# Reordered loads and weight folds, products of zeros ahead of the first load, and last sums chunk by chunk, in an FFT-attention and fp8 feed-forward kernel

## The chip, the cores and the metric

The kernel runs on one core of a Trainium2 chip. The metric is the time of one execution on the device in microseconds (us). A profile is of one such execution; its span is a little shorter than the execution's own time. In the profile PE is TensorE (matmuls), PEld its weight loads, DVE VectorE, ACT ScalarE, POOL GpSimd, and SP the engine that issues most DMAs.

## The reference

Four batches of 512 tokens of width 512 (x is 4x512x512, float32). First an attention without softmax, with 16 heads of 32 values:

```python
h = layernorm(x)
q  = (h @ W_q.T).reshape(B, S, 16, 32);  kv = (h @ W_kv.T).reshape(B, S, 16, 32)
qf = fft(q);  kvf = fft(kv)             # along a head's 32 values
qf = qf / l2norm(qf);  kvf = kvf / l2norm(kvf)
kvf = cumsum(kvf, axis=1)               # along the tokens of a batch
y = x + ifft(qf * kvf).real.reshape(B, S, 512) @ W_o.T
```

Then a feed-forward layer of inner width 1536, with weights rounded to fp8 (e4m3):

```python
h = layernorm(y)
g = silu((h @ fp8(gate_w)) * gate_scale);  u = (h @ fp8(up_w)) * up_scale
out = y + ((g * u) @ fp8(down_w)) * down_scale
```

## The kernel before, in words

The work is cut into 16 chunks of 128 tokens (N = 16, four to a batch). Nothing reorders it: the program is written out by hand, each engine executes its instructions in the order in which the Python code emits them, and Tile adds the semaphore waits.

**Loads.** SP issues in turn the first table `fwd` (L98), two of the four 128-row blocks of W_kv, the chunk x of 0, the identity table (L123), the other two blocks of W_kv, the transposed chunk xT of 0, then W_q, x and xT of 1, two more tables, and W_o (L115 to L130).

**Folds.** The real FFT is folded into the weights. `fold_in` (L162) multiplies 128x128 blocks of W_kv (tiles `pkv`) and W_q (tiles `pw`) by `fwd`: 16 products each, which PE executes as 32 instructions. `folded` (L172) copies the four sums to SBUF, two on ACT and two on DVE. `fold_out` (L176) folds the inverse transform into W_o in four 128x512 products, 8 instructions. Before, PE's order is W_kv, a quarter of W_q, chunk 0's `spectrum` with W_kv, the rest of W_q, W_o, and chunk 0's `spectrum` with W_q.

**A round of the attention.** For a chunk i:

- `x_mean`, `x_deviation` (ACT, with one power on POOL) give the layernorm; `x_row` (PE, L356) and `x_center` (DVE, L360) subtract the mean from xT;
- `spectrum(i, 1)` and `spectrum(i, 0)` (PE, L368, 8 instructions each) form k and q in the frequency domain; `squared` (ACT, L379), `summed` (DVE, L384) and `norms` (POOL, L389) their norms;
- `k_scaled` (DVE, L392) scales k and adds the carry of the chunk before; ACT copies the rounded high part `kh`, and `k_low` (DVE, L414) the remainder `kl`;
- `running` (PE, L423) sums along the tokens with a triangular matrix into `cum`; `carry` (ACT, L430, L431) copies the last row and sends it by a DMA to the next chunk; `q_scaled`, `products` (DVE, L440, L441) and `combined` (POOL, L449, L450) multiply the spectra;
- `v_out`, `v_back` take the product through DRAM, `v_turn` (DVE, L330) transposes it, `project` (PE, L467) multiplies it by the folded W_o, and `finish` (DVE, L475) adds x.

Chunks 0 to 2 are written out in a prologue (L601 to L684); the loop at L688 has one round for each of chunks 3 to 15, in which PE executes the two spectra of i, the running sum of i - 1 and the projection of i - 3.

**Rounding the weights.** The feed-forward weights come in 36 units, each rounded by ACT (`quant_abs`, L214) and by three or four parts on DVE (`next_parts`, L267): step, (floor), add and sub. `given` (L687) says how many parts a round has: 3 or 2. The prologue has four.

**Feed-forward.** 48 steps, 12 to a batch: `inner` (L532) forms 512 gate and up sums (16 matmuls each, `gu`), the product `f`, its rounded high part `fh` (ACT) and the remainder `fl` (DVE); `down` (L562) adds the step's share to four sums `pd`, one to a chunk, with 8 matmuls. For the last two steps `down` goes chunk by chunk. At a batch's end each chunk is scaled (DVE, L583), the residual added (POOL, or DVE for half of the last batch, L585) and stored (L586).

Of the kernel before, what the change touches and what calls it, by code (L numbers as in the profile page):

```python
# [15 lines left out]
P = 128  # L16
# [19 lines left out]
def tile_fft_attention_then_fp8_ffn(  # L36
# [54 lines left out]
    XB = 7  # L91
# [3 lines left out]


    tab = const.tile([P, 4, P], F32, name="tab")
    nc.sync.dma_start(tab[:, 0, :], tables[:, 0, :])  # L98
    fwd, ident, inv, tri = (tab[:, i, :] for i in range(4))

    xt, xTs = {}, {}
# [1 line left out]
    def load_xT(i):  # L103
        xTs[i] = work.tile([P, KC, P], F32, tag="xT", name=f"xT_{i}", bufs=3)
        nc.sync.dma_start(xTs[i], xT[i])

    def load_x(i):
        b, c = chunks[i]
        t = work.tile([P, D], F32, tag="x", name=f"x_{b}_{c}", bufs=XB)
        nc.sync.dma_start(t, x[b, c * P : (c + 1) * P, :])  # L110
        xt[i] = t
# [5 lines left out]
    for i, w in enumerate((w_kv, w_q, w_oT)):  # L117
        t = big_tile(f"raw{i}")
        for j in range(KC):
            nc.sync.dma_start(t[:, j, :], w[j * P : (j + 1) * P, :])  # L120
            if (i, j) == (0, 1):
                load_x(0)
                nc.sync.dma_start(tab[:, 1, :], tables[:, 1, :])  # L123
        raw.append(t)
        if i == 0:
            load_xT(0)
        elif i == 1:
            load_x(1)
            load_xT(1)
            nc.sync.dma_start(tab[:, 2:, :], tables[:, 2:, :])  # L130
# [28 lines left out]
    wq = big_tile("wq")  # L159
    wo = big_tile("wo")  # L160

    def fold_in(pw, r, j):  # L162
        for i in range(KC):
            nc.tensor.matmul(  # L164
                pw[i][:, j * P : (j + 1) * P],
                lhsT=r[:, j, i * P : (i + 1) * P],
                rhs=fwd,
                start=True,
                stop=True,
            )  # L170

    def folded(w, pw):  # L172
        for i in range(KC):
            (nc.scalar.copy, nc.vector.tensor_copy)[i % 2](w[:, i, :], pw[i])

    def fold_out(w, r):  # L176
        for j in range(KC):
            pw = ps.tile([P, D], F32, tag="acc", name="pw", bufs=4)
            nc.tensor.matmul(pw, lhsT=inv, rhs=r[:, j, :], start=True, stop=True)  # L179
            (nc.vector.tensor_copy, nc.scalar.copy)[j % 2](w[:, j, :], pw)  # L180


    U1 = 12
# [110 lines left out]

    def deviation(src, less, name):

        rstd = work.tile([P, 1], F32, tag="dev", name=f"dev_{name}", bufs=6)
        each = work.tile([P, D], F32, tag="each", name=f"each_{name}", bufs=1)
        nc.scalar.activation(each, src, AF.Square, bias=less, accum_out=rstd)  # L299
        nc.scalar.activation(rstd, rstd, AF.Identity, scale=1.0 / D, bias=eps)  # L300
        nc.gpsimd.tensor_tensor(rstd, rstd, nhalf[:, 0:1], ALU.pow)  # L301
        return rstd
# [40 lines left out]
    def x_mean(i):  # L343
        st_x[i] = lesses[i] = mean(xt[i], nm(i))
# [5 lines left out]
    def x_stats(i):  # L350
        x_mean(i)
        x_deviation(i)

    def x_row(i):
        rows[i] = ps.tile([P, KC, P], F32, tag="tp", name=f"row_{nm(i)}")
        nc.tensor.transpose(rows[i][:, 0, :], lesses[i].to_broadcast([P, P]), ident)  # L356

    def x_center(i):
        row = rows.pop(i)[:, 0:1, :].to_broadcast([P, KC, P])
        nc.vector.tensor_tensor(xTs[i], xTs[i], row, ALU.add)  # L360
# [51 lines left out]
    def k_low(i):  # L412
        kn, kh, kl = kns[i]
        nc.vector.tensor_tensor(kl, kn, kh.bitcast(F32), ALU.subtract)  # L414
# [113 lines left out]

    fused, pds = {}, {}
    STEPS = B * MC  # L530

    def inner(n, on_pe, on_act, between):  # L532
        b, m = divmod(n, MC)
        pgu = []
        for j, w in enumerate((wg, wu)):
            p = ps.tile([P, S], F32, tag="b", name=f"gu{j}_{b}_{m}")
            for k in range(KC):
                for v in (yhs[b], yls[b]):
                    nc.tensor.matmul(  # L539
                        p,  # L540
                        lhsT=w[:, k, m * P : (m + 1) * P],
                        rhs=v[:, k, :],
                        start=k == 0 and v is yhs[b],
                        stop=k == KC - 1 and v is yls[b],
                    )
            pgu.append(p)
            if j == 0:
                on_pe(n, 0)
        g = work.tile([P, S], F32, tag="tmp", name=f"g_{b}_{m}")
        nc.scalar.activation(g, pgu[0], AF.Silu, scale=gus[:, 0, m : m + 1])  # L550
        f = work.tile([P, S], F32, tag="qn", name=f"f_{b}_{m}")
        nc.vector.scalar_tensor_tensor(f, pgu[1], gus[:, 1, m : m + 1], g, ALU.mult, ALU.mult)  # L552
        on_act(n)
        fh = work.tile([P, S], F32R, tag="kh", name=f"fh_{b}_{m}", bufs=3)
        fl = work.tile([P, S], F32R, tag="kl", name=f"fl_{b}_{m}", bufs=3)
        nc.scalar.copy(fh, f)  # L556
        between(n)
        nc.vector.tensor_tensor(fl, f, fh.bitcast(F32), ALU.subtract)  # L558
        fused[n] = (fh, fl)
        on_pe(n, 1)  # L560

    def down(steps):  # L562

        b = steps[0] // MC
        if steps[0] % MC == 0:
            pds[b] = [
                ps.tile([P, D], F32, tag="acc", name=f"pd_{b}_{c}", bufs=4) for c in range(TC)
            ]
        for c in range(TC):
            for n in steps:  # L570
                m = n % MC
                for v in fused[n]:
                    nc.tensor.matmul(  # L573
                        pds[b][c],
                        lhsT=v[:, c * P : (c + 1) * P],
                        rhs=wd[:, m, :],
                        start=m == 0 and v is fused[n][0],
                        stop=m == MC - 1 and v is fused[n][1],
                    )
        if steps[-1] % MC == MC - 1:  # L580
            for c in range(TC):
                o = work.tile([P, D], F32, tag="x", name=f"o_{b}_{c}", bufs=XB)
                nc.vector.tensor_tensor(o, pds[b][c], dsc, ALU.mult)  # L583
                add = nc.vector if b == B - 1 and c % 2 else nc.gpsimd
                add.tensor_tensor(o, o, ys[b][:, c, :], ALU.add)  # L585
                nc.sync.dma_start(out[b, c * P : (c + 1) * P, :], o)  # L586


    def pair(n):
# [3 lines left out]
    def at(f, i, *more):  # L593
        if 0 <= i < N:
            f(i, *more)

    pkv = [ps.tile([P, D], F32, tag="acc", name=f"pkv{i}", bufs=4) for i in range(KC)]
    for j in range(KC):
        fold_in(pkv, raw[0], j)
    x_stats(0)  # L600
    x_row(0)  # L601
    folded(wkv, pkv)
    x_center(0)
    pw = [ps.tile([P, D], F32, tag="b", name=f"pw{i}") for i in range(2)]
    pw.append(ps.tile([P, D], F32, tag="tp", name="pw2"))
    pw.append(ps.tile([P, D], F32, tag="acc", name="pw3", bufs=4))
    fold_in(pw, raw[1], 0)
    x_stats(1)
    nc.vector.tensor_copy(tri_r, tri)

# [5 lines left out]
    spectrum(0, 1)  # L616
    squares(0, 1)
    norms(0, 1)
    for j in range(1, KC):
        fold_in(pw, raw[1], j)  # L620
    folded(wq, pw)
    x_row(1)
    x_center(1)
    quant_abs(0)
    k_scaled(0)
    fold_out(wo, raw[2])
    k_low(0)
    next_parts(1, True)
    spectrum(0, 0)
    squared(0, 0)  # L630
    running(0)
    carry(0)
    x_stats(2)
    next_parts(1, True)
    summed(0, 0)
    norms(0, 0)

    dsc = const.tile([P, D], F32, name="dsc")
    nc.sync.dma_start(gus[:, 0, :], gate_scale)
# [1 line left out]
    nc.sync.dma_start(dsc, down_scale.partition_broadcast(P))  # L641
    load_x(3)
    load_xT(3)
    spectrum(1, 1)
    squared(1, 1)
    x_row(2)
    x_center(2)
    summed(1, 1)
    norms(1, 1)
    q_scaled(0)  # L650
    products(0)
    combined(0)
    load_unit(wanted.pop(0))
    load_unit(3)
    v_out(0)
    spectrum(1, 0)
    squared(1, 0)
    x_mean(3)
    summed(1, 0)
    k_scaled(1)  # L660
    k_low(1)
    norms(1, 0)

    load_xT(4)
    load_x(4)
# [1 line left out]
    x_row(3)  # L667
    squared(2, 1)
    x_deviation(3)
    summed(2, 1)  # L670
    norms(2, 1)
    x_center(3)
    spectrum(2, 0)
    running(1)
    squared(2, 0)
    carry(1)
    x_mean(4)
    q_scaled(1)
    products(1)
    combined(1)  # L680
    v_back(0)
    summed(2, 0)
    norms(2, 0)
    next_parts(2, True)  # L684


    given = [2 if i in (6, 8, 10, 11, 12) else 3 for i in range(N - 3)] + [1, 0, 0]  # L687
    for i in range(3, N):  # L688

        at(load_xT, i + 2)  # L690
# [76 lines left out]
    def behind(n):  # L767
# [24 lines left out]
        if b + 1 < B and 0 <= m - 3 < TC:  # L792
            y_deviation(b + 1, m - 3)


    for n in range(STEPS + 1):
        if n < STEPS:
            inner(n, on_pe, on_act, between)
        if n == STEPS:
            down([n - 2, n - 1])  # L800
        elif n == STEPS - 1:
            down([n - 2])
        elif 0 < n < STEPS - 2:
            down([n - 1])
        if n < STEPS:
            behind(n)


def _tables():
# [61 lines left out]
```

## Time and profile before

| | |
|---|---|
| time, 3 runs | 464.65 to 465.56 us, median 465.56 us |
| the profiled execution's own time | 465.4 us |
| its span | 463.6 us |
| PE busy | 452.5 us (98%) in 1672 instructions |
| DVE busy | 280.9 us (61%) |
| ACT busy | 211.9 us (46%) |
| POOL busy | 192.6 us (42%) |
| spectrum, 8 instructions | 3.43 us of PE, one start to the next |
| one round of the attention, chunks 5 to 12 | 10.88 us of PE |
| one step of the feed-forward | 5.44 us of PE |

The profile lists for each engine its instructions with their start and length. A PE instruction is listed until its pipeline is empty, so a matmul's cost in a stream is the distance from its start to the next start. Times in the timeline count from the span's start.

### The profile page before, as it was taken

What the parts mean: (1) busy time and instruction counts of PE and PEld (TensorE: products, weight loads), DVE (VectorE), ACT (ScalarE), POOL (GpSimd) and SP (SyncE); (2) the same over time, 40 slices, a digit from 0 to 9 for tenths busy, and PEclk for the clock granted to TensorE, in tenths of its full rate; (3) what the DMA queues carried; (4) which work ended last, traced back from release to release, by engine and by line L of the source; (5) the groups of instructions that cost most, each with busy time, mean ns of one, the idle gap of its engine ahead of it and who ended that gap; (6) DMA issues with size and microseconds to landing.
All of it is one profiled execution on the core that took longest, in us unless ns stands there. A gap on an engine that the chain in (4) does not pass through costs nothing.

```text
span 463.6 us, 5026 instructions
## 1 busy us (share of the span) xinstructions
PE 452.5 (98%) x1672; PEld 308.5 (67%) x1672; DVE 280.9 (61%) x387; ACT 211.9 (46%) x428; POOL 192.6 (42%) x134
## 2 busy tenths in 40 slices
PE   6999999999999999999999999999999999999995
PEld 6544344444444444777788888888888888888883
DVE  1539898999888688798996342344433333522225
ACT  3663665656688433246943225533235432222220
POOL 0248888888899886510262140022301021400002
PEclk9999999999999999999999999999999999999999
DMA  8734366667645633662341050430141420200002
GB/s 290 278 113 137 91 159 160 183 178 216 193 126 154 163 77 85 189 207 91 101 105 23 0 182 22 92 69 0 45 138 30 100 53 1 91 1 0 0 1 90
DMA packets 82586, 49.13 MB, mean 106 GB/s; under 512 B 62080, under 2 KB 62464, under 8 KB 82560
## 3 DMA queue, kind: packets, MB, share of 16 engines
q1 hardware_dynamic: 82176, 48.79, 36.8%
q8 instruction: 13, 0.21, 0.2%
q14 instruction: 13, 0.11, 0.1%
q10 hardware_dynamic: 384, 0.03, 0.1%
HBM read 33.04 MB, written 15.73 MB: 105 GB/s over the span
## 4 chain that ended last, share of the span: by engine, by line
PE 92%; DVE 3%; ACT 3%; issue 1%; DMA 1%; ACTq 0%; SPq 0%; DVEq 0%
PE gu L539 38%; PE pq L368 19%; PE pd L573 19%; PE po L467 11%; PE cum L423 1%; PE pkv L164 1%; PE pw L179 1%; ACT sq L379 1%; PE pw L164 1%; ACT qm L222 1%; DMA raw<-in_w_kv 1%; ACT each L299 0%; ACT qa L221 0%; PE pt_f L317 0%; DVE ss L384 0%
## 5 line engine op out<-in xcount | busy, mean ns | idle before, releaser
L389 POOL TENSOR_TENSOR rn<-ss,nhalf 128x16 f32<-128x16 f32 x32 | 103.6, 3238 | 16.3 <-DVE ss L384 13.8
L552 DVE SCALAR_TENSOR_TENSOR f<-gu,gus,g 128x512 f32<-128x512 f32 x48 | 36.0, 750 | 108.5 <-PE gu L539 103.4
L539 PE MATMUL gu<-yh,wg 128*128 128x512 f32 x192 | 76.5, 398 | 0.0
L573 PE MATMUL pd<-wd,fl 128*128 128x512 f32 x192 | 74.8, 389 | 0.0
L539 PE MATMUL gu<-yl,wg 128*128 128x512 f32 x192 | 74.8, 389 | 0.0
L539 PE MATMUL gu<-yh,wu 128*128 128x512 f32 x192 | 74.7, 389 | 0.0
L573 PE MATMUL pd<-wd,fh 128*128 128x512 f32 x192 | 74.7, 389 | 0.0
L539 PE MATMUL gu<-yl,wu 128*128 128x512 f32 x192 | 74.7, 389 | 0.0
L556 ACT CAST fh<-f 128x512 fp32r<-128x512 f32 x48 | 29.8, 620 | 80.4 <-DVE f L552 80.4
L368 PE MATMUL pq<-wkv,xT 128*128 128x512 f32 x128 | 57.9, 595 | 1.3 <-DVE xT L360 1.3
L550 ACT ACTIVATE g<-gu,gus 128x512 f32<-128x512 f32 x48 | 33.0, 687 | 56.7 <-PE gu L539 56.4
L467 PE MATMUL po<-wo,qvT 128*128 128x512 f32 x128 | 57.6, 593 | 0.1
L368 PE MATMUL pq<-wq,xT 128*128 128x512 f32 x128 | 57.6, 592 | 0.0
L558 DVE TENSOR_TENSOR fl<-f,fh 128x512 fp32r<-128x512 f32 x48 | 35.8, 745 | 27.5 <-ACT fh L556 27.5
L585 POOL TENSOR_TENSOR o<-o,ys 128x512 f32<-128x512 f32 x14 | 17.7, 1291 | 81.7 <-DVE o L583 72.7
L368 PEld LDWEIGHTS pq<-wkv,xT 128*128 128x128 f32 x128 | 24.0, 190 | 31.1 <-issue 27.2
L301 POOL TENSOR_TENSOR dev_f<-dev_f,nhalf 128x1 f32<-128x1 f32 x16 | 12.5, 781 | 72.1 <-ACT dev_f L300 72.0
L368 PEld LDWEIGHTS pq<-wq,xT 128*128 128x128 f32 x128 | 23.2, 190 | 28.0 <-issue 27.2
L539 PEld LDWEIGHTS gu<-yh,wg 128*128 128x128 f32 x192 | 36.0, 188 | 8.7 <-issue 0.5
L539 PEld LDWEIGHTS gu<-yl,wg 128*128 128x128 f32 x192 | 36.0, 188 | 8.3 <-issue 0.7
L573 PEld LDWEIGHTS pd<-wd,fl 128*128 128x128 f32 x192 | 36.0, 188 | 7.7 <-DVE fl L558 0.2
L539 PEld LDWEIGHTS gu<-yh,wu 128*128 128x128 f32 x192 | 36.0, 188 | 7.5
(89 smaller groups left out, 609.6 us busy)
## 6 DMA issues: line engine op xcount, KB each, us to landing
x<-in_x SPq DMA_DIRECT2D x16, 256.0 KB, 3.2
xT<-in_xT SPq DMA_DIRECT2D x16, 256.0 KB, 3.1
qv_all<-qv SPq DMA_DIRECT2D x16, 256.0 KB, 4.4
zv<-qv_all SPq DMA_DIRECT2D x64, 64.0 KB, 2.6
y_all<-x SPq DMA_DIRECT2D x16, 256.0 KB, 2.3
ys<-y_all SPq DMA_DIRECT2D x16, 256.0 KB, 3.4
out<-o SPq DMA_DIRECT2D x16, 256.0 KB, 2.2
rawf<-in_gate_w SPq DMA_DIRECT2D x6, 512.0 KB, 4.8
```

The source lines that it names most:

```text
L164: nc.tensor.matmul(pw[i][:, j * P : (j + 1) * P], lhsT=r[:, j, i * P : (i + 1) * P], rhs=fwd, start=True, stop=True,)
L301: nc.gpsimd.tensor_tensor(rstd, rstd, nhalf[:, 0:1], ALU.pow)
L368: nc.tensor.matmul(pq, lhsT=xTs[i][:, k, :], rhs=w[:, k, :], start=k == 0, stop=k == KC - 1)
L389: nc.gpsimd.tensor_tensor(rns[i, j], sss.pop((i, j)), nhalf, ALU.pow)
L467: nc.tensor.matmul(po, lhsT=qvT[:, k, :], rhs=wo[:, k, :], start=k == 0, stop=k == KC - 1)
L539: nc.tensor.matmul(p, lhsT=w[:, k, m * P : (m + 1) * P], rhs=v[:, k, :], start=k == 0 and v is yhs[b], stop=k == KC - 1 and v is yls[b],)
L550: nc.scalar.activation(g, pgu[0], AF.Silu, scale=gus[:, 0, m : m + 1])
L552: nc.vector.scalar_tensor_tensor(f, pgu[1], gus[:, 1, m : m + 1], g, ALU.mult, ALU.mult)
L556: nc.scalar.copy(fh, f)
L558: nc.vector.tensor_tensor(fl, f, fh.bitcast(F32), ALU.subtract)
L573: nc.tensor.matmul(pds[b][c], lhsT=v[:, c * P : (c + 1) * P], rhs=wd[:, m, :], start=m == 0 and v is fused[n][0], stop=m == MC - 1 and v i ...
L585: add.tensor_tensor(o, o, ys[b][:, c, :], ALU.add)
```

## The change

- The two small tables go out on ACT's DMA queue ahead of its first instruction; W_kv is the first on SP's, whole, and x and xT of chunk 0 follow it.
- PE starts with eight 128x128 products of zeros (16 instructions) that write a tile nobody reads.
- W_q is folded as a whole before the first spectrum: two of its column blocks while W_kv's sums are copied, the other two into the buffers that come free.
- W_o is folded later: two products after chunk 1's second spectrum, two after chunk 2's, all four copied by ACT.
- The prologue has one rounding part where it had four, and the first `quant_abs` comes in chunk 2. The order of the small steps of chunks 0 to 2 is changed with it. `given` has 2 parts in rounds 3 and 10, and 3 in the rounds from 4 to 12 otherwise (before: 2 in 6, 8, 10, 11 and 12).
- At the end, `down` of the last four steps (LATE) is held back until all gates are done; then chunk 0 and 1, chunk 2, and chunk 3 in two halves of 256 columns. Each is scaled, added and stored by itself; only chunk 0's addition is left to POOL.
- The tile tag `dev` has 8 buffers where it had 6.

The diff, cut to its core:

```diff
-    nc.sync.dma_start(tab[:, 0, :], tables[:, 0, :])
+    nc.scalar.dma_start(tab[:, 0, :], tables[:, 0, :])
+    nc.scalar.dma_start(tab[:, 1, :], tables[:, 1, :])
...
             nc.sync.dma_start(t[:, j, :], w[j * P : (j + 1) * P, :])
-            if (i, j) == (0, 1):
-                load_x(0)
-                nc.sync.dma_start(tab[:, 1, :], tables[:, 1, :])
         raw.append(t)
         if i == 0:
+            load_x(0)
             load_xT(0)
...
+    def fold_out(w, r, j):
+        pw = ps.tile([P, D], F32, tag="tp", name=f"pwo{j}")
+        nc.tensor.matmul(pw, lhsT=inv, rhs=r[:, j, :], start=True, stop=True)
+        nc.scalar.copy(w[:, j, :], pw)
...
+    zero = work.tile([P, P], F32, tag="cross", name="zero", bufs=1)
+    nc.vector.memset(zero, 0.0)
+    idle = ps.tile([P, KC, P], F32, tag="tp", name="idle")
+    for n in range(8):
+        nc.tensor.matmul(idle[:, n % KC, :], lhsT=zero, rhs=zero, start=True, stop=True)
...
     x_stats(0)
-    x_row(0)
-    folded(wkv, pkv)
-    x_center(0)
+    for i in range(KC):
+        folded(wkv, pkv[i], i)
     pw = [ps.tile([P, D], F32, tag="b", name=f"pw{i}") for i in range(2)]
-    pw.append(ps.tile([P, D], F32, tag="tp", name="pw2"))
-    pw.append(ps.tile([P, D], F32, tag="acc", name="pw3", bufs=4))
-    fold_in(pw, raw[1], 0)
+    for j in range(KC):
+        for i in range(2):
+            fold_in(pw[i], raw[1], i, j)
+        if j == 0:
+            x_row(0)
+            x_center(0)
+    pw += [ps.tile([P, D], F32, tag="acc", name=f"pw{i}", bufs=4) for i in range(2, KC)]
+    for i in range(2, KC):
+        for j in range(KC):
+            fold_in(pw[i], raw[1], i, j)
+    for i in range(KC):
+        folded(wq, pw[i], i)
...
-    for j in range(1, KC):
-        fold_in(pw, raw[1], j)
-    folded(wq, pw)
     x_row(1)
     x_center(1)
-    quant_abs(0)
-    k_scaled(0)
-    fold_out(wo, raw[2])
-    k_low(0)
-    next_parts(1, True)
     spectrum(0, 0)
     squared(0, 0)
-    running(0)
-    carry(0)
-    x_stats(2)
-    next_parts(1, True)
     summed(0, 0)
     norms(0, 0)
+    k_scaled(0)
+    k_low(0)
...
+    x_stats(2)
     spectrum(1, 1)
     squared(1, 1)
+    summed(1, 1)
+    norms(1, 1)
+    running(0)
+    carry(0)
...
+    norms(1, 0)
+    fold_out(wo, raw[2], 0)
+    fold_out(wo, raw[2], 1)
     k_low(1)
...
     x_deviation(3)
+    quant_abs(0)
+    x_center(3)
     summed(2, 1)
     norms(2, 1)
-    x_center(3)
+    q_scaled(1)
+    running(1)
+    carry(1)
     spectrum(2, 0)
-    running(1)
...
+    next_parts(1, True)
+    load_unit(wanted.pop(0))
+    load_unit(3)
+    fold_out(wo, raw[2], 2)
+    fold_out(wo, raw[2], 3)
     summed(2, 0)
     norms(2, 0)
-    next_parts(2, True)
-    given = [2 if i in (6, 8, 10, 11, 12) else 3 for i in range(N - 3)] + [1, 0, 0]
+    next_parts(0, True)
+    given = [2 if i in (3,10) else 3 for i in range(N - 3)] + [1, 0, 0]
...
+    late = range(STEPS - LATE, STEPS)
+    b = B - 1
+    for c in range(2):
+        for n in late[:-1]:
+            down(n, [c])
+    down(late[-1], range(2))
+    for n in late:
+        down(n, [2])
+    halves = slice(0, D // 2), slice(D // 2, D)
+    for s in halves:
+        for n in late:
+            down(n, [3], s)
+    scaled_out(b, 0)
+    added_out(b, 0, nc.gpsimd)
+    scaled_out(b, 1)
+    added_out(b, 1, nc.vector)
+    scaled_out(b, 2)
+    added_out(b, 2, nc.vector)
+    for s in halves:
+        scaled_out(b, 3, s)
+        added_out(b, 3, nc.vector, s)
```

`scaled_out` is the multiplication of L583 and `added_out` the addition and the store of L585 and L586, for a chunk or a half of one. Where `down` is held back, the first late step's `fh` and `fl` use another tag (`qv`), so that all four steps' pairs stay in SBUF.

## The prediction

> **What bounds the kernel now.** I read the busy shares first, then the chain that ended last, then PE's timeline at both ends of the span.
>
> ```profile
> PE 452.5 (98%) x1672; PEld 308.5 (67%) x1672; DVE 280.9 (61%) x387; ACT 211.9 (46%) x428; POOL 192.6 (42%) x134
> ...
> PE 92%; DVE 3%; ACT 3%; issue 1%; DMA 1%; ACTq 0%; SPq 0%; DVEq 0%
> ```
>
> PE is the bound. The change takes no product away and adds sixteen instructions, so it can win only where PE waits, where it runs slowly, or after its last product. PE's timeline shows such places in the first 53 us:
>
> ```profile
> 3.75 6.42 PE L164 MATMUL pkv<-tab,raw 128*128 128x128 f32 x32 [3.75 <-DMA raw<-in_w_kv]
> 10.02 0.27 PE L356 MATMUL row<-tab,less 128*128 128x128 f32 x1
> 10.12 1.06 PE L164 MATMUL pw<-tab,raw 128*128 128x128 f32 x8
> 11.71 3.70 PE L368 MATMUL pq<-wkv,xT 128*128 128x512 f32 x8 [0.53 <-DVE xT L360]
> 15.25 2.84 PE L164 MATMUL pw<-tab,raw 128*128 128x128 f32 x24
> 17.92 0.27 PE L356 MATMUL row<-tab,less 128*128 128x128 f32 x1
> ```
> ```profile
> 39.81 0.40 PE L423 MATMUL cum<-kl,tri_r 128*128 128x512 f32 x1
> 40.77 3.70 PE L368 MATMUL pq<-wkv,xT 128*128 128x512 f32 x8 [0.57 <-DVE xT L360]
> ...
> 47.83 0.49 PE L423 MATMUL cum<-kh,tri_r 128*128 128x512 f32 x1
> 48.56 0.50 PE L423 MATMUL cum<-kl,tri_r 128*128 128x512 f32 x1 [0.23 <-DVE kl L414]
> 49.18 3.70 PE L467 MATMUL po<-wo,qvT 128*128 128x512 f32 x8
> 53.12 3.70 PE L368 MATMUL pq<-wkv,xT 128*128 128x512 f32 x8 [0.24 <-DVE xT L360]
> ```
>
> Three losses. **Waiting for the load**: nothing until 3.75. **Slow products**: W_kv's 32 instructions take 10.02 - 3.75 = 6.27 us, W_q's 24 of the same shape 17.92 - 15.25 = 2.67 (0.107 each after a restart of 0.1). The granted clock reads 1.00 throughout, but the weight loads show it: median 333 ns under `pkv`, 192 under `pw`. At half speed, 0.213, until a switch: 6.27 = 0.213n + 0.107(32 - n) gives n = 27, so the rate changed 5.7 us after the first product. **Stalls**: from 10.02 to 53.12 are 43.1 us. The work there is eight spectra of 3.43, W_o 3.43 and a projection 3.43 (8 x 0.43 each), W_q 3.42, five rows of 0.11, three running sums of 0.46: 39.65. So 3.45 are stalls, most at 10.98 (0.7), 20.8 (0.3), 40.0 (0.7), 48.3 (0.9) and 52.7 (0.5). From 53 on I found only 0.3 us, near 222 to 233 and 454.7.
>
> The end, after PE's last product:
>
> ```profile
> 457.53 0.39 PE L573 MATMUL pd<-wd,fl 128*128 128x512 f32 x1
> 457.74 1.27 DVE L583 TENSOR_TENSOR o<-pd,dsc 128x512 f32<-128x512 f32 x2
> 458.50 1.26 POOL L585 TENSOR_TENSOR o<-o,ys 128x512 f32<-128x512 f32 x1 [1.23 <-DVE o L583]
> 459.05 1.26 DVE L585 TENSOR_TENSOR o<-o,ys 128x512 f32<-128x512 f32 x1
> ```
>
> PE ends at 457.92; DVE still scales chunks 2 and 3 and adds chunk 3 until 460.31; issue, landing and the end take 3.3 more.
>
> **Loads and zeros.** Engines are released at 0.72 (SP's first issue). The zeros need one memset on DVE, whose first work today is at 9.77; POOL's memsets take 0.10, so PE starts near 0.95. Nothing hides behind it but the load. Sixteen instructions at 0.213 end at 4.35, when the tables (landing 3.0 after issue) and the first block of W_kv (issued at 0.72 for 1.16) are there. `pkv` thus starts 0.6 later than today. If the rate changes 5.7 us after the first product again, at 6.65, 11 instructions are slow and 21 fast (2.27): `pkv` ends at 8.9, against 10.02. Bounds: if zeros do nothing, 4.35 + 6.27 = 10.6; if all are fast, 7.8.
>
> Then W_q: 4 instructions, the row, 12 instructions, then 16 into buffers that ACT's and DVE's copies free at 9.6 (x of 0, issued after W_kv, lands near 6.8; ACT's statistics take 2.1 and two copies 1.1). The sum is 8.9 + 0.43 + 0.11 + 1.28 + 1.71 = 12.45. A floor stands beside it: W_q's last block is issued some 0.7 earlier than today's 5.9 and lands 4.7 later (median of W_q's loads), at 9.9 to 10.3; 0.43 + 1.71 after that is 12.4 at the latest. So earlier warmth would gain little more, and both bounds are 12.4 and 14.1.
>
> The Trainium skill ("DMA: Bandwidth & Descriptors", Issuing engines are not separate DMA queues) speaks against moving the tables: all queues end on the same 16 DMA engines, and a second issuer saves only the sequencer's time. The trace has one issue at 0.44 us, so by the page the move is worth at most two of them; my sum needs no more. On the slow rate its page "TensorE: Matmul & The Clock Gate" (What's actually happening) says that a free-running window of 3.4 us has to be busy, so a switch comes 3.4 to 6.8 us after the first product, and 5.7 agrees; by it `pkv` ends between 7.8 and 9.1, whatever the zeros hold.
>
> **Folds and the prologue.** At 12.45 W_kv is copied and x_center done (DVE: two copies to 10.1, center to 10.8), so the stall at 10.98 is gone: `spectrum(0,1)` runs to 15.9. W_q's copies end at 13.1, inside it. `spectrum(0,0)` ends at 19.4, `spectrum(1,1)` at 22.8. What is late next is chunk 0's `kl`: square to 16.7, sum 17.3, the power on POOL 2.9 to 20.3, the other sum 20.9, `kn` 21.6, `kh` 22.25, `kl` 22.95: even with PE (0.1). Chunk 1's: `squared(1,1)` queues on ACT behind chunk 2's statistics to 25.1, POOL to 28.8, `kn` and carry to 31.1, `kh`, `kl` to 32.45. PE has by then done `spectrum(1,0)`, two W_o products and `spectrum(2,1)`, to 32.1, and waits 0.4. The other two W_o products fill the gap before round 3. On ACT `quant_abs(0)` (1.08 + 1.27 + 0.25 = 2.6) now stands ahead of `carry(1)`; who waits: the carry's DMA, `kn`, `kh` and `kl` of chunk 2, at 43.0, which PE wants at 45.2. That cover is 2.2 us. `v_turn(0)` is done at 43.7, `x_center(4)` at 47.5, wanted at 45.7 and 49.1. SP's order hurts nobody: unit 2's loads, behind `v_back(0)`, are read a round later.
>
> Sum: 12.45 + work left (39.65 - 3.42 - 0.11 = 36.1) + stalls 0.6 = 49.2 for round 4's start, against 53.12: **-3.9**. The stalls have no row; bounds are 0, and the prologue's present 2.7 after 12 us.
>
> **Rounding.** Parts are on DVE, off the path; three leave the prologue, and rounds 6, 8, 11 and 12 gain a third. From one `kn` to the next those rounds have 9.1 to 9.4 us of DVE work today, and a part is 0.6 (step) to 1.3; 10.3 to 10.6 against PE's 10.88, as in a three-part round today:
>
> ```profile
> 85.86:96.74 10.88, 10.53 (x15) 1.00 0.55 151
> ```
>
> DVE enters round 4 at 50.6, 1.4 us after PE, where today it is 3.2 behind. I take 0; without that cover every microsecond over 10.88 is PE's.
>
> **The end.** Same products; one chunk is cut in halves. The last `fl` came 2.4 us after the last gate sum today; twelve products (2.7) now stand between, so no stall. Sixteen half products: nearest rows are 0.107 for a 128-column float32 instruction and 0.227 for a 512-column one; I take 0.12, +0.1 in all (bounds: 0, and 188 ns of weight load each, +1.2). In the instruction list the second half's scaling has no wait on PE of its own, so the first half's waits for the last product: the halves don't overlap PE. After it DVE has four half operations of 0.4 (rows L449 and L450, 128x240) with no POOL beside them: 1.7 + 3.3 = 5.0, against 463.6 - 457.9 = 5.7. Chunks 0 to 2 are done before. Net **-0.5**.
>
> Sum: -3.9 - 0.5 = -4.4 against the execution's own 465.4, which is 0.16 below the median: **461.0**.
>
> **Rivals.**
>
> 1. The zeros warm nothing (too early, or an idle window between). Then `pkv` ends at 10.6: +1.7, 462.7. For: the clock row says nothing. Against: the slow rate here ended by itself under products. 15%.
> 2. A wait replaces the stalls: ACT, with squares, statistics, `quant_abs` and copies in one queue, makes chunk 1's and 2's `kl` late by 2 us more. For: the 0.4 above and ACT's order. 463.0. 10%.
> 3. Slower: DVE becomes the bound in the nine rounds from 4 to 12. Its waits for POOL's power (0.8 and 1.3 before `qn` at 102 and 145) are today in two-part rounds, which absorb them; if they stay beside a third part, a round is 10.6 + 1.05 = 11.65: 9 x 0.77 - 1.4 = 5.5, 466.5. It decides from 11.5 a round. 5%.
> 4. The change doesn't do what it says: already counted for the halves; for the rest the instruction lists show the new order.
>
> **The numbers.** Forecast 461.0 with 65%, itself 459.9 (no new stalls, an early warm clock, end -0.7) to 462.2; small remaining mixtures of lost gains 5%, near no change. The range 459.9 to 463.1 takes in rivals 1 and 2. 0.2% (0.93 us) is what a measurement of this kernel can tell from no change: faster 0.89, same 0.05, slower 0.06.
>
> **What would show it.** PE from about 1.0; `pkv` over before 9.1; `spectrum(0,1)` near 12.4; round 4 at 49 and then 10.88 a round; a last product near 454, four short DVE operations, and 5.0 us from there to the end. Wrong if `pkv` is slow to the end, if `cum` waits on `kl` for microseconds, if rounds 6 to 12 stretch, or if half products take 0.19.

## The result and the profile after

The changed kernel takes **461.14 us** (median of 6 runs, 460.43 to 461.81); the kernel before, 465.15 us (6 runs beside it, 464.53 to 465.56). The ratio is 0.9915, with a 95% interval of 0.9900 to 0.9929: faster by 4.0 us. Its profiled execution took 460.43 us, with a span of 458.6 us, against 465.4 and 463.6 before.

The busy shares and the first line of the chain that ended last, after:

```profile
PE 452.7 (99%) x1696; PEld 310.9 (68%) x1696; DVE 280.0 (61%) x389; ACT 213.0 (46%) x430; POOL 189.0 (41%) x133
...
PE 99%; DVE 0%; issue 0%; DVEq 0%
```

PE is listed as busy as long as before, 452.7 us against 452.5, in a span that is 5.0 us shorter; some 3.6 us of it are now the zeros. The chain, which held 3% each of DVE and ACT before, is PE alone. So the gain is time in which PE stood still or ran slowly, and no product is saved.

PE's timeline of the first 20 us, after (start, busy us, line, operation):

```profile
1.03 3.78 PE L607 MATMUL idle<-zero 128*128 128x128 f32 x16 [1.03 <-DVE zero L604]
4.61 4.43 PE L162 MATMUL pkv<-tab,raw 128*128 128x128 f32 x32
8.88 0.61 PE L162 MATMUL pw<-tab,raw 128*128 128x128 f32 x4
9.33 0.27 PE L352 MATMUL row<-tab,less 128*128 128x128 f32 x1
9.44 3.46 PE L162 MATMUL pw<-tab,raw 128*128 128x128 f32 x28
12.73 3.60 PE L364 MATMUL pq<-wkv,xT 128*128 128x512 f32 x8
```

W_kv's fold starts 0.86 us later than before, at 4.61, and is over 1.14 us earlier, at 8.88. It takes 4.27 us. With 0.2125 us for a slow instruction and 0.107 for a fast one, 4.27 = 0.2125n + 0.107(32 - n) gives about 8 slow ones where there were 27. PE's rate changed near 6.3, 5.3 us after its first product.

The end of the prologue, after:

```profile
44.88 0.79 PE L419 MATMUL cum<-kh,tri_r 128*128 128x512 f32 x1
45.51 0.39 PE L419 MATMUL cum<-kl,tri_r 128*128 128x512 f32 x1
45.74 3.59 PE L463 MATMUL po<-wo,qvT 128*128 128x512 f32 x8
49.17 2.31 PE L364 MATMUL pq<-wkv,xT 128*128 128x512 f32 x5
```

No line ends in a bracket: the waits that stood at 40.77, 48.56 and 53.12 before are gone, and round 4 starts at 49.17 in place of 53.12. From there to PE's last product 404.6 us pass, 404.8 before. The rest of the gain is behind that product (DVE's and PE's rows at the end):

```profile
453.47 0.28 PE L572 MATMUL pd<-wd,fl 128*128 128x256 f32 x1
453.84 0.43 DVE L586 TENSOR_TENSOR o<-pd,dsc 128x256 f32<-128x256 f32 x1 [0.29 <-PE pd L572]
454.30 0.42 DVE L590 TENSOR_TENSOR o<-o,ys 128x256 f32<-128x256 f32 x1
454.65 0.42 DVE L586 TENSOR_TENSOR o<-pd,dsc 128x256 f32<-128x256 f32 x1
455.10 0.43 DVE L590 TENSOR_TENSOR o<-o,ys 128x256 f32<-128x256 f32 x1
```

PE ends at 453.75 and the span at 458.6: 4.85 us, against 5.68 before. Both halves are scaled after PE's last product. Between the profiled executions the change is 3.95 us up to round 4, 0.2 in the stream and 0.8 at the end, 5.0 in all; the medians differ by 4.0. After's profiled execution is the fastest of its six, 0.7 below their median, and before's lies 0.25 above its own.

How far one profile can be trusted shows in the experiments' profiles. Those that keep after's prologue and its eight zeros (e3, e8, e9, e10, e12) start the first spectrum between 13.16 and 13.59, after at 12.73. From the first spectrum to round 4 they all take 36.4 us, after too. So these profiles differ from after's in what lies ahead of the first spectrum, and what an edit behind it is worth is best read from there to the end of the span: 445.9 us in after (458.6 - 12.73).

### The profile page after: what moved, and what is told of

It is laid out like the page before. It is cut to its first block, busy times and chain, and to the rows that moved or that the text cites. A ratio compares the mean times of both kernels' runs of the same rounds, so it can differ in the third digit from the quotient of the medians.

```text
span 458.6 us, 5066 instructions
## 1 busy us (share of the span) xinstructions
PE 452.7 (99%) x1696; PEld 310.9 (68%) x1696; DVE 280.0 (61%) x389; ACT 213.0 (46%) x430; POOL 189.0 (41%) x133
## 4 chain that ended last, share of the span: by engine, by line
PE 99%; DVE 0%; issue 0%; DVEq 0%
PE gu L536 38%; PE pq L364 24%; PE pd L572 19%; PE po L463 12%; PE cum L419 2%; PE pkv L162 1%; PE idle L607 1%; PE pw L162 1%; PE pwo L175 1%; PE row L352 0%; PE pt_f L313 0%; DVE o L590 0%; DVE o L586 0%; DVE zero L604 0%; DVEq L586 0%
## 5 line engine op out<-in xcount | busy, mean ns | idle before, releaser
L385 POOL TENSOR_TENSOR rn<-ss,nhalf 128x16 f32<-128x16 f32 x32 | 104.7, 3273 | 17.3 <-DVE ss L380 16.1
L572 PE MATMUL pd<-wd,fh 128*128 128x512 f32 (+1 forms) x196 | 75.1, 385 | 0.0
L572 PE MATMUL pd<-wd,fl 128*128 128x512 f32 (+1 forms) x196 | 75.0, 385 | 0.0
L590 POOL TENSOR_TENSOR o<-o,ys 128x512 f32<-128x512 f32 x13 | 16.4, 1292 | 79.0 <-DVE o L586 70.1
L536 PEld LDWEIGHTS gu<-yh,wg 128*128 128x128 f32 x192 | 36.1, 188 | 8.7 <-issue 0.7
L572 PEld LDWEIGHTS pd<-wd,fh 128*128 128x128 f32 x196 | 36.8, 188 | 7.4
```

The costliest lines, as they stand in the source:

```text
L385: nc.gpsimd.tensor_tensor(rns[i, j], sss.pop((i, j)), nhalf, ALU.pow)
L536: nc.tensor.matmul(p, lhsT=w[:, k, m * P : (m + 1) * P], rhs=v[:, k, :], start=k == 0 and v is yhs[b], stop=k == KC - 1 and v is yls[b],)
L572: nc.tensor.matmul(pds[b][c][:, s], lhsT=v[:, c * P : (c + 1) * P], rhs=wd[:, m, s], start=m == 0 and v is fused[n][0], stop=m == MC - 1 a ...
L590: add.tensor_tensor(o, o, ys[b][:, c, s], ALU.add)
```

## The experiments

Theory: four things give the gain, and their shares add up: the zeros (PE reaches its full rate earlier), the order of loads and folds and the place of the rounding (no stalls in the prologue), and the chunk-wise end. Rivals: the zeros do nothing, and the loads' order does their work; or the gain at the end comes from the held-back steps alone, and the halves add nothing. Times are medians, ratios are to the kernel before run beside each. That the shares simply add up fell with e5. No run takes the order of loads and folds back alone.

### Without the zeros: e1_no_zeros

```diff
-    zero = work.tile([P, P], F32, tag="cross", name="zero", bufs=1)
-    nc.vector.memset(zero, 0.0)
-    idle = ps.tile([P, KC, P], F32, tag="tp", name="idle")
-    for n in range(8):
-        nc.tensor.matmul(idle[:, n % KC, :], lhsT=zero, rhs=zero, start=True, stop=True)
```

> The changed kernel without the products of zeros. Theory (the zeros pay because they use up the slow time while the load is awaited): the folds of W_kv start with the load near 3.7 us, their 32 instructions are again slow for some 5.5 us, they end near 9.8 instead of 8.9; part of that is hidden behind W_q's load, so 0.7 to 1.0 us longer than the changed kernel's 461.1: about 462.0. Rival (the zeros only delay, and the folds became faster for another reason, for example because the load no longer competes): the folds start 0.9 earlier and are as fast as in the changed kernel, 460.3 to 461.1.

461.54 us (461.18 to 462.03), ratio 0.9924 [0.9911, 0.9937]. The fold's row in its timeline:

```profile
4.13 6.18 PE L162 MATMUL pkv<-tab,raw 128*128 128x128 f32 x32 [4.13 <-DMA tab<-in_tables]
```

About 27 instructions are slow again, with the change of rate 5.7 us after the first product. The first spectrum starts at 13.84, round 4 at 50.27: 1.1 us later than in after's profile, but 0.3 to 1.1 later than in the eight profiles with after's loads and eight zeros (12.71 to 13.59). The median is 0.4 longer, less than the 0.7 to 1.0 expected, and the two intervals overlap: from this run alone the zeros' gain isn't clear of noise. `pkv` waits here for the tables, until 4.13, where the kernel before waited for W_kv until 3.75. So in this profile the tables, moved to ACT's queue, didn't come earlier; behind eight zeros that doesn't show, and no run takes the move back alone.

### The kernel before with the zeros: e2_only_zeros

The same five lines are added to the kernel before, ahead of `pkv`.

> The kernel before with the eight products of zeros and nothing else. Theory: the folds of W_kv end 1.0 us earlier, and the old order of PE then waits as long as before, so the time falls by about 0.9: 464.2. Rival (the zeros help only with the new order, because in the old one x of chunk 0 and its centering come last anyway): 465.1, no change.

464.48 us (463.86 to 464.78, 11 runs), ratio 0.9984 [0.9976, 0.9993]: -0.7 us. `pkv` runs from 4.61 to 9.27 (before: 10.02), and then PE waits 0.38 us for W_q, which this kernel still loads late:

```profile
9.92 1.16 PE L164 MATMUL pw<-tab,raw 128*128 128x128 f32 x8 [0.38 <-DMA raw<-in_w_q]
```

The first spectrum starts at 10.96 (before: 11.71), round 4 at 52.35 (53.12). So the zeros work by themselves, and what they win is capped by the next load.

### Five and sixteen products of zeros: e6_five_zeros, e7_sixteen_zeros

```diff
-    for n in range(8):
+    for n in range(5):
```

and `range(16)` in e7.

> The changed kernel with five products of zeros for eight. Theory: they end near 3.2, the folds start at the load near 3.7, the rate changes at the same 6.3 to 6.7, so the folds end near 8.5, and W_q's load then sets the pace: 460.8 to 461.1, the same as the changed kernel. Rival (the half microsecond of idling, or the shorter run, puts the change of rate off): the folds end near 9.9, 462.0.

461.57 us (460.54 to 462.03), ratio 0.9924 [0.9910, 0.9937]. The zeros end near 3.2, `pkv` runs from 3.79 to 9.13 with about 18 slow instructions, and round 4 starts at 49.24, beside after's 49.17. The rate changes near 7.6, later than the 6.3 to 6.7 expected, and the fold ends between what the theory (8.5) and the rival (9.9) said; the median is 0.4 above after's, inside both kernels' ranges.

> The changed kernel with sixteen products of zeros for eight. Theory: 32 instructions, slow until 6.3 to 6.7 and fast from there, end near 7.1; all folds are then fast and W_kv's end near 10.5; W_q's follow, 1.4 us later than in the changed kernel: 462.4. Rival 1 (products of zeros do not warm the clock): the zeros take until 7.9, W_kv's folds are slow behind them and end near 13.9: 466. Rival 2 (the load sets the pace in any case): 461.1.

461.74 us (461.09 to 462.60), ratio 0.9929 [0.9916, 0.9943]. Its first rows:

```profile
1.04 5.27 PE L607 MATMUL idle<-zero 128*128 128x128 f32 x32 [1.04 <-DVE zero L604]
6.15 3.74 PE L162 MATMUL pkv<-tab,raw 128*128 128x128 f32 x32
```

32 instructions took 5.11 us (6.15 - 1.04), not 32 x 0.213 = 6.8, so about half were already fast; `pkv` is fast from its first instruction (9.72 - 6.15 = 3.57 us). PE executed nothing but zeros before: products of zeros do bring the full rate. The extra eight keep `pkv` waiting until 6.15, and round 4 starts at 49.84, no later than in some of the profiles with eight (49.61 to 50.02). The median is 0.6 above after's where 1.3 was expected. Between five and sixteen the number matters by some tenths of a us, within the runs' spread.

### The old end: e3_old_tail

Steps are held back only for the last two, all four chunks are whole, and every second addition is POOL's, as before:

```diff
-    LATE = 4
+    LATE = 2
...
+    for c in range(TC):
+        for n in range(STEPS - LATE, STEPS):
+            down(n, [c])
+    for c in range(TC):
+        scaled_out(b, c)
+        added_out(b, c, nc.vector if c % 2 else nc.gpsimd)
```

> The changed kernel with the last sums of the kernel before (two late steps, whole chunks, additions of chunks 0 and 2 on POOL). Theory: from PE's last product to the end 5.7 us instead of 4.85, less 0.1 for the half products: 0.7 longer than the changed kernel's 461.1, 461.8. Rival (the end gained nothing, all came from the first 50 us): 461.1.

461.93 us (461.54 to 462.57), ratio 0.9928 [0.9915, 0.9940]: +0.8. Its last product ends at 454.31, its span at 459.9: 5.6 us behind PE, against 4.85. From the first spectrum to the end it takes 446.7 us, against 445.9. That is the predicted kind and size. The run takes three things back at once (held-back steps, halves, POOL's share of the additions), so it doesn't say which of them pays.

### Chunk 3 in one piece, and its halves in two banks: e8_whole_chunk, e9_two_banks

```diff
-    halves = slice(0, D // 2), slice(D // 2, D)
+    halves = (slice(0, D),)
```

> The changed kernel with chunk 3 of the last batch whole instead of in halves, all else as changed. Theory (the halves do not overlap PE, since the first half's scaling waits for the last product): after PE one scaling of 0.68 and one addition of 0.68 instead of four operations that take 1.69 together, and 0.1 less of products: 0.3 to 0.4 shorter than 461.1, 460.75. Rival (the halves pay, because the first half's store goes out earlier and the last is half as large): 461.5.

460.86 us (460.78 to 461.39), ratio 0.9906 [0.9893, 0.9920]: 0.3 below after, as expected in size, but inside the intervals. DVE's rows behind its last product, which ends at 454.59:

```profile
454.68 0.69 DVE L586 TENSOR_TENSOR o<-pd,dsc 128x512 f32<-128x512 f32 x1 [0.20 <-PE pd L572]
455.40 0.69 DVE L590 TENSOR_TENSOR o<-o,ys 128x512 f32<-128x512 f32 x1
```

Two whole operations take 1.41 us from first start to last end, four halves 1.69. But behind DVE's last operation the span goes on for 3.5 us, with halves for 3.1, and from the first spectrum to the end it is 446.0 us against 445.9. So neither the theory's gain nor the rival's loss of 0.4 is there: with the halves the end comes sooner behind DVE's last operation, by about what DVE's two more operations cost. Cutting chunk 3 buys nothing here, since its first half isn't scaled beside PE.

e9 gives the second half a PSUM tile of its own (`pd_own`), so that the first half waits for its own products alone:

```diff
+                for t, o in split(b, c, s):
                     nc.tensor.matmul(
-                    pds[b][c][:, s],
+                    pds[b][t][:, o],
```

> The changed kernel with the second half of the last batch's chunk 3 summed in a PSUM tile of its own, in all twelve steps of that batch. Theory: the first half is scaled and added beside PE's last eight products, and two operations of 0.43 stand behind PE instead of four: 0.8 shorter at the end; eight more steps with four half products for two whole ones cost 8 x 0.025 = 0.2: 0.6 shorter than 461.1, 460.5. Rival (DVE still waits for PE's last product): 461.3.

461.16 us (460.96 to 462.16), ratio 0.9915 [0.9901, 0.9928]: no gain, so the expectation failed. The first half is scaled at 454.37, as PE's last product starts, since DVE is busy with chunk 2 until then:

```profile
454.37 0.41 DVE L597 TENSOR_TENSOR o<-pd,dsc 128x256 f32<-128x256 f32 x1
```

The chunk is cut in all twelve steps of the batch, so that PE pays for the halves more often: from round 4 to its last product's end 405.0 us pass, against 404.6. PE ends at 454.65, with only 4.45 us behind it: what is won at the end is lost in the stream.

### The old places of the rounding: e4_old_rounding

After, with the first `quant_abs`, the prologue's four parts, the loads of two units and `given` where they were before; loads, folds, zeros and end as after.

```diff
     x_center(1)
+    quant_abs(0)
     spectrum(0, 0)
...
     k_low(0)
+    next_parts(1, True)
...
     x_stats(2)
+    next_parts(1, True)
     spectrum(1, 1)
...
-    next_parts(0, True)
+    next_parts(2, True)
-    given = [2 if i in (3,10) else 3 for i in range(N - 3)] + [1, 0, 0]
+    given = [2 if i in (6, 8, 10, 11, 12) else 3 for i in range(N - 3)] + [1, 0, 0]
```

> The changed kernel with the rounding as it was: the first quantization before chunk 0's second spectrum, four parts in the prologue, the old list of parts to a round. Theory (the parts in the prologue were part of the old stalls): the second unit's quantization on ACT, 2.6 us, stands ahead of chunk 1's squares, chunk 1's high and low parts come 2 us later and PE waits for them: 1.5 to 2.5 longer than 461.1, about 463.0. Rival (the old stalls came from the order of the folds alone): 461.1.

**467.43 us** (467.19 to 467.85), ratio 1.0048 [1.0034, 1.0062]: 6.3 above after, where 1.5 to 2.5 was expected, and slower than the kernel before. PE stands still in the prologue (rows shown below, with e11), and round 4 starts at 52.92, 3.75 late. The other 3 us are in the feed-forward: each steady step takes 5.52 us in place of 5.44, though PE's instructions are the same in the same order, nothing waits, and the granted clock is 1.00. No step of the theory has that. Later experiments take the two apart.

### The kernel before with the rounding moved: e5_only_rounding

The reverse of e4's edit, on the kernel before: no `quant_abs(0)` ahead of chunk 0's second spectrum, one part in the prologue, the change's `given`.

> Before with one part of the change alone: the first rounding of weights (quant_abs(0) and its parts) moved out of rounds 0 to 2 to the places the change gives it, and the parts of rounds 4 to 12 shared out as the change does; loads, order of the folds, tail and the missing zeros stay as before. Theory (the rounding's ACT and DVE work delays what PE waits for at 40.0, 48.3 and 52.7 us of before's trace; undoing its move cost 3.75 us up to round 4): at least the half of that comes back from before's side too, round 4 starts near 51.2 in place of 53.1 and the time is 463.3 (462.6 to 464.0). Rival (the place of the rounding hurts only together with the new order of the folds, where output folds stand in rounds 1 and 2): round 4 at 53.1, time 465.1. The spacing of the feed-forward's products is read as well: 0.2267 us if it has nothing to do with where tiles lie, since the tiles lie at other places here than in either kernel.

**468.70 us** (467.9 to 469.4), ratio 1.0072 [1.0054, 1.0090]. Both expectations miss. The row of PE that waits most in its prologue:

```profile
46.19 0.32 PE L356 MATMUL row<-tab,less 128*128 128x128 f32 x1 [1.26 <-ACT less L292]
```

Moved into chunk 2 without the new order of the folds, ACT's rounding stands ahead of chunk 4's mean, and PE waits for that. Round 4 starts at 54.74, 1.6 later than before; half of this isn't the edit's, for W_kv's load comes later in this profile and the first spectrum starts at 12.53 (before: 11.71). The rival was nearer: the place of the rounding has a value only together with the order of the rest. The other part is in the stream again: from round 4 to the end of PE's last product 404.8 us became 406.2.

### Only the places of tiles: e10_moved_tiles, e11_old_rounding_places, e12_moved_f

Where a tile lies in SBUF follows from the order in which the tags are first allocated, and e4 allocates the rounding's tags earlier. e10 is after with the same instructions in the same order on all five engines, and the working tiles where e4 has them; unused tiles do it:

```diff
     x_center(1)
+    for n in range(2):
+        work.tile([P, QH, D], F32, tag="qa", name=f"qa_p{n}")
+        work.tile([P, QH, D], F32, tag="qm", name=f"qm_p{n}")
+        work.tile([P, 1], F32, tag="qc", name=f"qc_p{n}")
     spectrum(0, 0)
```

> After, with the same instructions in the same order on all five engines, but with the small working tiles at the places in SBUF that they have in the kernel with the old rounding (e4): the rounding's tags are allocated earlier, by unused tiles of the same size, which nothing writes or reads. Theory (the 3.0 us that e4 lost in the feed-forward, 5.52 us a step in place of 5.44, come from where its tiles lie): the steps take 5.52 us, the prologue is as after's (round 4 near 49.2), time 464.1. Rival (they come from something else in e4, the timing of its weights' rounding or the state the prologue leaves behind): steps of 5.44 us, time 461.1.

**464.18 us** (463.69 to 464.47, 12 runs), ratio 0.9975 [0.9966, 0.9983]: +3.0 us by places alone. PE's groups between 240 and 450 us (busy us, mean ns of one):

```profile
L536 PE MATMUL gu<-yh,wg 128*128 128x512 f32 x156 | 61.4, 394 | 0.0
...
L536 PE MATMUL gu<-yh,wu 128*128 128x512 f32 x156 | 60.7, 389 | 0.0
...
L572 PE MATMUL pd<-wd,fh 128*128 128x512 f32 x146 | 58.2, 398 | 0.0
```

In after every such group has a mean of 389 ns. In after the last of these groups reads:

```profile
L572 PE MATMUL pd<-wd,fh 128*128 128x512 f32 x153 | 59.5, 389 | 0.0
```

From start to start, a product with `fh` takes 0.236 us in e10 and 0.227 in after; the last column shows no wait.

e11 is e4 with after's places (unused tiles of the tags `ss0`, `rn0`, `kn`, `kh`, `kl`, `end`, `qn` and `qv` ahead of `quant_abs(0)`).

> The kernel with the old rounding (e4), with the same instructions in the same order, but its small working tiles at the places that they have in after. Theory of places: steps of 5.44 us, round 4 still near 52.9, time 464.4. Rival (the cause is in the order of the rounding): steps of 5.52 us, time 467.4. Between the two: both have a share, and their shares are read from the steps here and in the kernel sent beside it.

**464.11 us** (464.00 to 464.65, 12 runs), ratio 0.9975 [0.9967, 0.9984]. The stream is back at 5.44 us a step, and the prologue's stalls stay, with round 4 at 53.36. PE's waits in e11:

```profile
PE row L352 <- ACT wo L176: 1.4, 1, 1.4
PE idle L607 <- DVE zero L604: 1.0, 1, 1.0
PE pwo L175 <- DVE xT L356: 0.8, 1, 0.8
PE cum L419 <- ACT kh L405: 0.8, 1, 0.8
PE cum L419 <- DVE kl L410: 0.2, 1, 0.2
```

After has the second line alone. So taking the rounding's place back costs 3.0 us in the median (464.11 against 461.14), at equal places of tiles. In the profiles it is 4.0 us from the first spectrum to round 4 (40.4 against 36.4).

e12 halves the set of e10: `fh` and `fl` (with `kn`, `kh`, `kl`) lie as in after, `f`, `qn`, `qv` and `end` as in e10.

```diff
     k_scaled(0)
+    for n in range(2):
+        work.tile([P, QH, D], F32, tag="qa", name=f"qa_p{n}")
...
     k_low(0)
```

> After's instructions in after's order once more; fh and fl (and kn, kh, kl) lie where after has them, but f, qn, qv and end lie where e10 has them (16.4 kB per partition further on), with the rounding's tiles between the two. It halves the set of tiles that e10 moved at a cost of 3.0 us. Theory (the slow products are those of pd, which load fh and fl, and those of wg, which run while ACT and DVE write fh and fl; so the place of fh and fl decides): feed-forward steps of 5.44 us, time 461.1. Rival (the place of f or of qn and qv decides): steps of 5.52 us, 464.2.

461.05 us (460.75 to 461.31), ratio 0.9912 [0.9898, 0.9925], after's time. The same two groups in e12:

```profile
L536 PE MATMUL gu<-yh,wg 128*128 128x512 f32 x156 | 60.7, 389 | 0.0
...
L572 PE MATMUL pd<-wd,fh 128*128 128x512 f32 x152 | 59.2, 389 | 0.0
```

The place of `fh` and `fl` decides, or something that lies with them (`ss0`, `rn0`, `kn`), which the feed-forward doesn't use; not that of `f`, `qn`, `qv` and `end`.

## Why the prediction was right, point by point

- **Sum.** 461.0 forecast, 461.14 measured as the median. That they lie so close is in part luck: the profiled execution took 460.43, and its gain was 3.95 up to round 4 (3.9 forecast), 0.2 in the stream (none forecast) and 0.8 at the end (0.5). With round 4 at 49.6 to 50.0, as in the other profiles with the same prologue, the first term is 3.1 to 3.5. Three parts taken back alone give 0.4 (zeros, e1), 0.8 (end, e3) and 3.0 us (rounding, e11 against after), 4.2 against the 4.0 gained. That is no proof of separate shares: the order of loads and folds has no figure of its own, and the rounding's move by itself made the kernel before slower (e5).
- **Zeros.** Start 0.95 forecast, 1.03 measured; `pkv` from 4.35 and 4.61, until 8.9 and 8.88; rate change 5.7 and 5.3 us after the first product. Right in the profile, and e7 shows that zeros warm PE. But 5.7 isn't a constant. In the profiles of the kernels with zeros it comes between about 3.3 (e4, e7) and 6.6 us (e6) after the first product, and `pkv` with eight products ahead takes 3.6 to 4.7 us. (The counts of slow instructions are good to one or two: e7's fold, all fast, takes 3.57 where 32 x 0.107 are 3.42.) The Trainium skill ("TensorE: Matmul & The Clock Gate", What's actually happening) has a free-running window of 3.4 us, one of which must be busy; an estimate from it is 3.4 to 6.8 us, which these runs agree with. The prediction's latest end of `pkv` by that page, 9.1, is a slip: a change 6.8 us after 0.95 gives 9.5, and e9 has 9.31. In the same text the page's spread for the moment is ±500 ns; here it is three times that.
- **Floor by W_q's load.** It is real, and lies later than the 12.4 "at the latest" of the prediction. In e10 the rate changes early, and the fold of W_kv is over at 8.36:

```profile
8.81 0.71 PE L162 MATMUL pw<-tab,raw 128*128 128x128 f32 x4 [0.45 <-DMA raw<-in_w_q]
9.47 3.85 PE L162 MATMUL pw<-tab,raw 128*128 128x128 f32 x28
```

Yet its first spectrum starts at 13.16, 0.4 later than after's: the 28 last instructions of `pw` take 3.7 us and not 3.0, since PE's weight loads wait for W_q's blocks one after the other. They do so in e3, e4, e8 and e12 too (0.6 to 1.1 us in all, with a wait ahead of `pw` in some). In e6, where `pkv` ends only at 9.13, the first spectrum starts at 12.81. So with zeros ahead, an early change of rate doesn't bring an early first spectrum. Why W_q's blocks land at different times is open. After's own first spectrum started at 12.73 against 12.45, since these 28 instructions took 3.29 us.
- **Prologue.** Round 4 at 49.2 forecast, 49.17 measured; this 0.03 is luck, as five more profiles with the same prologue have it at 49.61 to 50.02. The chain of chunk times holds: `kl` of chunks 0, 1 and 2 done at 23.35, 32.71 and 43.37 (22.95, 32.45, 43.0 forecast), `x_center(4)` at 47.0 (47.5). Stalls from the first spectrum on are 49.17 - 12.73 - 36.1 = 0.3 us, where 0.6 was taken.
- **Rounding.** "I take 0" for nine rounds with a third part held: 10.87 a round. From 70.91 to 81.78 DVE has 10.75 us of work, the most of the eight rounds after 60.04, and PE is never late. What the prediction had too small is what this part is for: it counted the rounding's move into the stalls' end and gave it no figure of its own; taken back alone, it costs 3.0 us (e11).
- **End.** Half products 0.12 apart, as taken; DVE four halves behind PE, as read from the instruction list; 4.85 us against 5.0. By the prediction's own terms (0.7 less behind PE, 0.1 more of products) the net is -0.6 and not -0.5; the profiles have -0.8. e8 shows that whole operations are no worse.
- **Rivals.** 1 (zeros warm nothing) fell with e7. 2 (ACT's queue) didn't occur in after, but it is the mechanism of e4, e5 and e11, with 1.3 to 1.4 us for its longest wait. 3 (DVE bound) didn't occur. 4 named the halves, which don't overlap PE; that was in the sum, and it came out.
- **What no step had**: the change also moved tiles in SBUF. It went well here; with e4's places it would have given back three quarters of the gain.

e12, e8 and e9 are level with after within the intervals; no run was clearly faster than it.

## What to carry to other kernels

Where one engine is busy 98% of the time, look for its idle time by place, and write down when each input is due and when it is made; that table gave the new start of the stream to within 1 us in every profile of this prologue. Then read an edit from a point behind the part that differs between executions: here 0.9 us of difference lay ahead of the first spectrum, more than several of the edits were worth. An order of small steps is worth something as a whole: undo a part in both directions before giving it a share. And after any edit of the allocation order, compare the spacing of the same instruction in the steady stream; if it moved without a wait, hold the places fixed with unused tiles before explaining the time by the edit.

## What the runs showed that was not expected

- **PE's products take 0.227 us or up to 0.236 with the same instructions, depending on where tiles lie in SBUF** (e10 against after, 3.0 us in 464). Of the moved tiles, `fh` and `fl` are read by PE as weights and written by ACT and DVE. The products that read them are slowed (0.236 with `fh`, 0.230 with `fl`), and also the first six of the eight with `wg` behind them (in the mean 0.231 with `yh`, 0.229 with `yl`); products with `wu` are not. The Trainium skill ("SBUF — State Buffer", Who interferes with whom) says that only the port pair of VectorE and GpSimd causes contention and that PE never waits on anyone. If the cause here is contention, these runs speak against that; that it is isn't shown, for the profile names no wait, and a weight load takes 188 ns in e10 as in after. What rule of addresses decides is open: `fh`'s first buffer begins at byte 194,560 of a partition in e10 and e4, at 178,112 in after and e12 and at 192,192 in the kernel before (0.227 us in all three), and at 175,744 in e5 (1.4 us longer from round 4 to the end of PE's last product).
- **PE runs at half rate for about 3.3 to 6.6 us after its first product while the granted clock reads 1.00.** The spacing of equal instructions shows it, 0.213 against 0.107 us.
